# Zero products on TensorE ahead of the first weights, and the first loads of a decoder layer in halves

## The chip, the cores and the metric

The kernel runs on one core of one Trainium2 chip. The metric is the device time of one execution in microseconds (us). The core has five engines that run side by side, each with its own instruction queue: TensorE (PE in the profile, its weight loads as PEld), VectorE (DVE), ScalarE (ACT), GpSimd (POOL) and SyncE (SP). [...]DMA transfers between device memory and the on-chip buffers are issued from the queues of SP, ACT and POOL.

## What is computed

One post-norm decoder layer in float32 for 8 sequences of 112 tokens with 256 channels. The parts follow each other:

```
x = layernorm(x + self_attention(x))            # 16 heads of 64, w_qkv 256 x 3072, w_out 1024 x 256, bias
x = layernorm(x + cross_attention(x, context))  # 16 heads of 16, context of 375 rows, mask, biases
x = layernorm(x + moe(x))                       # 8 experts, hidden 512, each token to its best one,
                                                # and one shared expert for all tokens
```

The first thing that can be computed is the projection of x to queries and keys: `x @ w_qkv`, the columns 0 to 1023 for q and 1024 to 2047 for k. Only this beginning of the kernel is touched by the change.

## The kernel before, in words

The host lays x out transposed (`in_xT`, 256 x 896), so that the channel is the partition; 256 channels make two chunks of 128, called k (KD = 2). The three parts of `w_qkv` are three tiles `wq`, `wk`, `wv` of 128 partitions x 2 chunks x 1024 columns.

The order of the work is written out by hand. Inside `tc.manual_schedule()` each engine executes what the program issues, in program order; the tables FIRST, STEP, STEP6, STEP7 and LAST are lists of short words, and `step` runs them one after the other. A word such as `k6` or `u0-` is one piece: some matmuls into one PSUM tile and the copy out of it (`+` by DVE, `-` by ACT).

The beginning goes like this.

- Loads. `load` is SP's DMA start, `A.dma_start` is ACT's. L131 loads the columns of x of the first two sequences (both chunks in one transfer, 224 KB). `load_w(start, n, c, width)` (L128 and L129) loads `width` columns of q, k or v (n = 0, 1, 2) from column c, for both chunks. L132 to L138: q's columns 0 to 255 from ACT's queue, k's 0 to 255 from SP, q's 256 to 511 from ACT, k's 256 to 511 from SP, then from SP q's, k's and v's remaining halves of 512 columns each. After them SP issues the context of sequence 0, the cross-attention weights and biases, the rest of `xT` (L158), the residual x, the output weights and more (L153 to L167).
- Constants. POOL makes the identity for the transposes, a few small tiles and zeros in two wide tiles; DVE makes three tiny vectors (L177 to L180). TensorE has nothing to do before the first projection.
- First pieces. L559 and L560 run the four pieces k0 to k3 of `project(0, 0)`: k0 is q's columns 0 to 255, k1 is k's columns 0 to 255, k2 and k3 the same for columns 256 to 511. One piece is four calls of `nc.tensor.matmul` in `product` (L246 to L248): two column blocks of 128, called i here, each summed over the two chunks. Then ACT scales q into `qT` (L273), or DVE copies k into `kT` (L244). The trace shows two TensorE instructions for each such call in float32, so eight for a piece.
- Then the table FIRST: `k6 k4 u0- k5- k7+ s0 e0 s1 k3- ...`. Here k4 to k7 are the other halves of the projection of sequences 0 and 1, u0 is half of the values of sequence 0, s0 and s1 are the scores of the self attention. A later `k3` is already a piece of the next pair of sequences and reads the rest of `xT`.

All matmul pieces of this kind draw their PSUM tile from `m_tile` (L97), a pool with two buffers.

Eight sequences then go through the steps, with the self attention of one sequence laid between the cross attention of the one before. The loads of later contexts wait for a free buffer, so for TensorE's progress. The end (LAST) is the routing, the experts, the shared expert and the last norm.

Of the kernel before, what the change touches and what calls it, by code (L numbers as in the profile page):

```python
# [8 lines left out]
F32 = mybir.dt.float32  # L9
# [5 lines left out]
P = 128  # L15
# [38 lines left out]
def decoder_layer(  # L54
# [8 lines left out]
    nc = tc.nc  # L63
    B, S, D = x.shape
    NT = B * S
    S2 = ctxT.shape[1] // B
    KD = D // P
# [6 lines left out]
    E, _, H = upT.shape  # L74
# [14 lines left out]
    V, A, G = nc.vector, nc.scalar, nc.gpsimd  # L89
# [7 lines left out]
    def m_tile():  # L97
        return ps_m.tile([P, 512], F32, tag="mm", name="mm")
# [10 lines left out]
    ac = sa.enter_context(tc.tile_pool(name="ac", bufs=1))  # L109
# [3 lines left out]
    xT_sb = ac.tile([P, KD, NT], F32, name="xT_sb")  # L113
# [10 lines left out]
    load = nc.sync.dma_start  # L124
    xT_v = xT.rearrange("(k p) n -> p k n", p=P)
    w_v = w_qkv.rearrange("(k p) n -> p k n", p=P)

    def load_w(start, n, c, width):  # L128
        start(out=wqkv[n][:, :, bass.ds(c, width)], in_=w_v[:, :, bass.ds(n * INNER + c, width)])  # L129

    load(out=xT_sb[:, :, 0 : 2 * S], in_=xT_v[:, :, 0 : 2 * S])  # L131
    load_w(A.dma_start, 0, 0, 256)  # L132
    load_w(load, 1, 0, 256)
    load_w(A.dma_start, 0, 256, 256)
    load_w(load, 1, 256, 256)
# [426 lines left out]
    for s in range(B):  # L562
        if s + 1 < B:
            load_context(s + 1)
        if s in (1, 2):
            load(
                out=(xs_d if s == 1 else y_d)[:, :].rearrange("(t p) d -> p t d", p=P),
                in_=fill_sb.unsqueeze(1).to_broadcast([P, E * NT // P, D]),
# [409 lines left out]
```

## Time and profile before

| what | value |
|---|---|
| median of the 3 runs | 417.99 us (417.88 to 418.55) |
| the profiled execution's own time | 418.89 us |
| its span in the trace | 417.2 us |
| TensorE busy | 399.4 us, 96% of the span |
| VectorE, ScalarE, GpSimd busy | 58%, 45%, 18% |
| first TensorE instruction | 5.11 us after the span's start |

The span is what lies between the first and the last record of the trace; the profiled execution's own time is 1.7 us more. In the profile a line such as "5.11 3.36 PE L248 MATMUL ... x8" reads: from 5.11 us, for 3.36 us, eight matmuls issued by line 248; in brackets stands how long the engine had been idle and what released it. PEld is the loading of weights into the array, which runs beside matmuls. "128*128 128x224" means stationary 128 x 128, output 128 partitions x 224 columns. SPq and ACTq are the queues that issue DMAs.

### The profile page before, as it was taken

What the parts mean: (1) busy time and instruction counts of PE and PEld (TensorE: products, weight loads), DVE (VectorE), ACT (ScalarE), POOL (GpSimd) and SP (SyncE); (2) the same over time, 40 slices, a digit from 0 to 9 for tenths busy, and PEclk for the clock granted to TensorE, in tenths of its full rate; (3) what the DMA queues carried; (4) which work ended last, traced back from release to release, by engine and by line L of the source; (5) the groups of instructions that cost most, each with busy time, mean ns of one, the idle gap of its engine ahead of it and who ended that gap; (6) DMA issues with size and microseconds to landing.
All of it is one profiled execution on the core that took longest, in us unless ns stands there. A gap on an engine that the chain in (4) does not pass through costs nothing.

```text
span 417.2 us, 8496 instructions
## 1 busy us (share of the span) xinstructions
PE 399.4 (96%) x3347; PEld 311.2 (75%) x3347; DVE 239.9 (58%) x672; ACT 188.2 (45%) x476; POOL 75.3 (18%) x111
## 2 busy tenths in 40 slices
PE   5999999999999999999999999999999989999991
PEld 4877768967886887688678867867857559998670
DVE  0173585578458665865784587489487424223173
ACT  1232366455727554654567286577476221112000
POOL 3012112103012200221030112104100520000271
PEclk9999999999999999999999999999999999999998
DMA  8980298099010001000000100000694140995132
GB/s 273 309 224 0 78 376 293 4 362 353 26 37 2 2 1 38 2 2 8 31 2 2 38 0 2 2 2 2 218 373 167 46 142 4 304 358 174 45 107 60
DMA packets 38334, 46.61 MB, mean 112 GB/s; under 512 B 2181, under 2 KB 31378, under 8 KB 38290
## 3 DMA queue, kind: packets, MB, share of 16 engines
q1 hardware_dynamic: 36978, 43.66, 32.2%
q0 software_dynamic: 768, 1.84, 1.5%
q8 instruction: 28, 0.46, 0.5%
q10 hardware_dynamic: 544, 0.52, 0.4%
q14 instruction: 16, 0.13, 0.1%
HBM read 28.41 MB, written 17.60 MB: 110 GB/s over the span
## 4 chain that ended last, share of the span: by engine, by line
PE 86%; POOL 4%; issue 4%; DMA 3%; DVE 2%; ACT 0%; SPq 0%; POOLq 0%; DVEq 0%
PE mm L248 46%; PE pt L485 10%; PE sc L248 7%; PE sc L437 7%; PE mm L496 5%; PE sc L336 4%; PE mm L372 3%; PE pt L365 3%; POOL r L677 1%; POOL xs_d L664 1%; DMA wq<-in_w_qkv 1%; POOL rs L229 1%; PE pt L239 1%; DMA xs_d<-xres,place_i 1%; DMA xs<-xs_d 1%
## 5 line engine op out<-in xcount | busy, mean ns | idle before, releaser
L455 ACT ACTIVATE ex<-ex,nm 112x375 f32<-112x375 f32 x128 | 76.8, 601 | 47.3 <-DVE nm L451 46.5
L451 DVE CUSTOM_DVE_ANT_0 ex<-sc,cap 112x375 f32<-112x375 f32 x128 | 63.7, 545 | 10.0 <-PE sc L437 9.6
L485 PEld LDWEIGHTS pt<-ident,ex 112*125 112x125 f32 x384 | 50.9, 188 | 17.2 <-issue 10.0
L485 PE MATMUL pt<-ident,ex 112*125 112x112 f32 x384 | 55.1, 275 | 0.1
L244 ACT COPY exT<-pt 125x448 f32<-125x448 f32 x56 | 28.4, 528 | 29.1 <-PE pt L485 29.0
L358 POOL TENSOR_TENSOR pr<-pr,den 112x896 f32<-112x896 f32 x16 | 26.9, 1684 | 80.9 <-DVE den L357 44.2
L229 POOL TENSOR_TENSOR rs<-rs,mhalf 112x1 f32<-112x1 f32 x24 | 13.4, 560 | 144.6 <-DVE rs L228 144.5
L248 PE MATMUL mm<-xT_sb,wq 128*128 128x224 f32 x128 | 28.9, 373 | 5.1 <-DMA wq<-in_w_qkv 5.1
L248 PE MATMUL mm<-wv,xT_sb 128*112 128x512 f32 x64 | 31.1, 608 | 0.0
L248 PEld LDWEIGHTS mm<-xT_sb,wq 128*128 128x128 f32 x128 | 24.4, 199 | 8.5 <-DMA wq<-in_w_qkv 5.1
L437 PE MATMUL sc<-kc,qz 32*112 32x375 f32 x256 | 29.8, 519 | 0.1
L248 PE MATMUL mm<-wo,aoT 128*112 128x256 f32 x128 | 29.0, 380 | 0.0
L244 DVE COPY exT<-pt 125x448 f32<-125x448 f32 x40 | 24.8, 623 | 7.0 <-PE pt L485 6.5
L248 PE MATMUL mm<-xT_sb,wk 128*128 128x224 f32 x128 | 28.0, 364 | 0.0
L248 PEld LDWEIGHTS mm<-xT_sb,wk 128*128 128x128 f32 x128 | 24.8, 198 | 1.7 <-issue 0.5
L248 PE MATMUL mm<-wxv,cT 128*125 128x256 f32 x96 | 25.6, 389 | 0.0
L248 PEld LDWEIGHTS mm<-wo,aoT 128*112 128x112 f32 x128 | 22.0, 177 | 4.5 <-DVE aoT L244 0.2
L455 ACT ACTIVATION_READ_ACCUMULATOR ex<-ex,nm 112x1 f32 x128 | 24.1, 188 | 0.0
L248 PE MATMUL mm<-cT,wxk 128*128 128x375 f32 x64 | 23.2, 486 | 0.0
L244 DVE COPY prT<-pt 112x448 f32<-112x448 f32 x16 | 9.9, 621 | 20.7 <-PE pt L365 20.7
L496 PE MATMUL mm<-exT,vc 125*32 125x112 f32 x768 | 21.7, 261 | 0.0
L345 DVE TENSOR_REDUCE mx<-sc 112x8 f32<-112x896 f32 x16 | 17.4, 1088 | 5.8 <-PE sc L336 5.3
(156 smaller groups left out, 641.1 us busy)
## 6 DMA issues: line engine op xcount, KB each, us to landing
xs_d<-fill_sb SPq DMA_DIRECT2D x1, 7168.0 KB, 24.2
y_d<-fill_sb SPq DMA_DIRECT2D x1, 7168.0 KB, 24.9
wg<-in_gateT SPq DMA_DIRECT2D x9, 512.0 KB, 8.5
wu<-in_upT SPq DMA_DIRECT2D x9, 512.0 KB, 7.5
wd<-in_downT SPq DMA_DIRECT2D x9, 512.0 KB, 8.0
cT<-in_ctxT SPq DMA_DIRECT2D x8, 375.0 KB, 3.6
wv<-in_w_qkv SPq DMA_DIRECT2D x2, 512.0 KB, 7.8
wo<-in_w_out SPq DMA_DIRECT2D x1, 1024.0 KB
```

The lines of the kernel that those rows point to most:

```text
L229: G.tensor_tensor(rs[:n], rs[:n], mhalf[:n], ALU.pow)
L244: (V.tensor_copy if on == "+" else A.copy)(dst, src)
L248: nc.tensor.matmul(out_, lhsT, rhs, start=(i == 0), stop=(i == len(pairs) - 1))
L336: nc.tensor.matmul(sc[:S, j, bass.ts(c, S)], qT[rows, 4 * g + c, self.tok], kT[rows, 4 * g + c, self.tok], start=True, stop=True,)
L345: V.tensor_reduce(self.mx, scv, AX.X, ALU.max)
L358: G.tensor_tensor(pr, pr, den.unsqueeze(3).to_broadcast([S, 2, 4, S]), ALU.mult)
L365: nc.tensor.transpose(pt[:S, bass.ts(c, S)], self.pr[g][:, j, c, :], ident[:S, :S])
L437: nc.tensor.matmul(sc[i // 2][:S, i % 2, :S2], self.qz[rows, par, c, :], kc[rows, c, :], start=True, stop=True,)
L451: V.tensor_tensor_reduce(ex[:, i, :], self.sc[g][i // 2][:S, i % 2, :S2], cap, -1.0, BIG, ALU.add, ALU.min, nm[:, i : i + 1],)
L455: A.activation(ex[:, i, :], ex[:, i, :], AF.Exp, bias=nm[:, i : i + 1], scale=-1.0, accum_out=den[:, i, g % 2 : g % 2 + 1],)
L485: nc.tensor.transpose(pt[:JT, bass.ts(i, S)], self.ex[g][:, i, bass.ts(t, JT)], ident[:S, :S])
L496: nc.tensor.matmul(av[32 * i : 32 * i + 32, 0:S], vcs[self.b % 2][:, t, 4 * c + i, bass.ds(32 * par, 32)], self.exT[2 * c + par][:, t, bas ...
```

## The change

Ahead of all loads a tile of 128 x 128 zeros is allocated, VectorE fills it, and TensorE multiplies it with itself seven times into a PSUM tile of `m_tile` that nobody reads. Then the first loads are issued in smaller parts and in another order: q's first 256 columns become two transfers of 128 columns (both from ACT's queue), and the columns of x for the first two sequences become two transfers, one for each chunk (both from SP's queue). All other loads follow as they were. Nothing else in the kernel is changed.

```
-    load(out=xT_sb[:, :, 0 : 2 * S], in_=xT_v[:, :, 0 : 2 * S])
-    load_w(A.dma_start, 0, 0, 256)
+
+    zeros = ac.tile([P, P], F32, name="zeros")
+    V.memset(zeros, 0.0)
+    idle = m_tile()
+    for _ in range(7):
+        nc.tensor.matmul(idle[:, :P], zeros, zeros, start=True, stop=True)
+
+    load_w(A.dma_start, 0, 0, P)
+    for k in range(KD):
+        load(out=xT_sb[:, k, 0 : 2 * S], in_=xT_v[:, k, 0 : 2 * S])
+    load_w(A.dma_start, 0, P, P)
     load_w(load, 1, 0, 256)
     load_w(A.dma_start, 0, 256, 256)
     load_w(load, 1, 256, 256)
```

## The prediction

> **What bounds the kernel now.** I read the page first, then the chain of waits in order of time for the first 60 us, then the timeline of the first 20 us, then the tables by stretches of the start and of the end, and the waits of TensorE over the whole span. The page:
>
> ```profile
> PE 399.4 (96%) x3347; PEld 311.2 (75%) x3347; DVE 239.9 (58%) x672; ACT 188.2 (45%) x476; POOL 75.3 (18%) x111
> PE 86%; POOL 4%; issue 4%; DMA 3%; DVE 2%; ACT 0%; SPq 0%; POOLq 0%; DVEq 0%
> ```
>
> TensorE is busy 96% of the span and carries 86% of the chain that ends last: time taken off TensorE's own work or off its start comes off the end, unless something takes its place. Two pieces of the chain and two waits of TensorE tell where it starts:
>
> ```profile
> 0.81 4.25 DMA wq<-in_w_qkv
> 5.11 16.73 PE mm L248 x68
> ...
> PE mm L248 <- DMA wq<-in_w_qkv: 5.1, 1, 5.1
> PE pt L800 <- DMA xs<-xs_d: 1.1, 2, 0.9
> ```
>
> The first weights of q end the wait at 5.11; after that TensorE waits for a DMA only near the end, 1.1 us. What it does from 5.11 on is the key to this change:
>
> ```profile
> 5.11 3.36 PE L248 MATMUL mm<-xT_sb,wq 128*128 128x224 f32 x8 [5.11 <-DMA wq<-in_w_qkv]
> 8.26 2.79 PE L248 MATMUL mm<-xT_sb,wk 128*128 128x224 f32 x8
> 10.89 1.68 PE L248 MATMUL mm<-xT_sb,wq 128*128 128x224 f32 x8
> 12.40 1.68 PE L248 MATMUL mm<-xT_sb,wk 128*128 128x224 f32 x8
> ```
>
> Four pieces of eight equal matmuls start at 5.11, 8.26, 10.89, 12.40, and the fifth at 13.91. The distances are 3.15, 2.63, 1.51, 1.51. No wait is shown inside, and yet the first two take 1.64 and 1.12 us more: 2.76 us. In the first, an instruction takes about 0.37 us, from 10.70 on 0.19: TensorE runs at half rate for 5.6 us. The clock column doesn't say so:
>
> ```profile
> 5.00:8.00 3.00, 2.89 (x8) 2.63 (x9) 0.00 (x0) 0.00 (x0) 0.00 (x0) 1.00 1.08 368
> ...
> 412.00:414.00 2.00, 0.00 (x0) 0.00 (x0) 0.00 (x0) 0.00 (x0) 0.00 (x0) 0.82 0.26 71
> 414.00:417.20 3.20, 0.00 (x0) 0.00 (x0) 0.00 (x0) 0.00 (x0) 0.00 (x0) 0.50 0.02 4
> ```
>
> (columns: length, PE, PEld, DVE, ACT, POOL, granted clock, DMA share, GB/s.) It shows 1.00 at 5 to 8, where the intervals are doubled, but at the end, with TensorE idle from 408.2, it falls to 0.50 (at 413.3 in finer stretches). So 0.5 is this engine's clock when it has been idle, and 1.00 at the start I read as "no record yet".
>
> [...]
>
> **The change part by part.**
>
> *Zeros.* VectorE's fill of 128x128: POOL's of the same shape took 0.205 us, DVE has nothing before its first instruction at 1.55. From 0.8, so ready at about 1.0. Seven calls are 14 instructions (a piece of four calls shows eight). The nearest row is wxq's projection, 128*128 with 112 columns, eight in 0.88 us (46.19 to 47.07): 0.11 us each at full clock, 0.13 scaled to 128 columns, doubled while cold: 0.22 to 0.25, so 3.1 to 3.5 us, from about 1.1 to 4.2 or 4.6. This lies in the 5.1 us in which TensorE waits, so it costs nothing if the first operands arrive at 4.5; without that cover it would be 3.3 us. DVE's three tiny vectors move by 0.2 us; they are read by the queries at about 46. The unread PSUM tile shifts the turn of the two buffers; the piece that gets it back is on TensorE too, in order behind it, so nothing.
>
> [...]
>
> *The halves.* The first matmul now needs 128 KB of q and 112 KB of x, instead of 256 and 224. In fine stretches DMA moves 292 GB/s at 3.0 to 3.4 and some 375 after it; summed to 5.07 that is about 830 KB, of which 490 are the two tiles and the rest other loads. Half of it is reached at 4.0. The bounds are 4.0 and 5.07; I take 4.5. But this serves only the first of four calls: the second needs the other chunk of x, the third the other half of q, and these come when the undivided ones came, about 5.0 to 5.1; later, up to 5.8, if transfers with half as long rows (512 bytes, which no row of this trace has) get a smaller share beside SP's. So the halves themselves move one or two instructions, 0.2 to 0.4 us, and nothing if the clock is up, since the next tile then decides.
>
> *What is late next.* k1 needs wk's first part. It was issued at 1.33 and landed at 6.1 (4.8 us later); SP now issues one transfer more ahead of it (0.46 us), so 6.1 to 6.6. Before, it was wanted at 8.26, so it was hidden; now it decides. After it the weights come faster than they are used: 256 KB each 0.7 us against 1.51 us of work. q's second half landed near 8.6 and is wanted about 11; v's first landed near 11.4, wanted about 14; the rest of xT landed at 10.04 + 8.6 = 18.6, wanted at 23.53, now 20.7. Slack of about 2 us each. The SP queue's own waits (SPq L157, L158, ... one landing each) are those of eight transfers in flight; the two added ones are early in that row, so from bk on each issue waits for the same landing as before. ACT issues one DMA more (0.5 us), so its table load ends at 3.7, not 3.2; its first use was at 8.50, now about 6.5.
>
> [...] I charge the issue of 0.46 us only.
>
> *Sum.* Clock up by about 5: k0 from 4.5, ends with q's second half near 6.2; k1 from 6.4, then 1.51 each: k6 at 10.95 against 13.91, gain 2.95. Clock up at 7.2: k0 from 4.5 cold, 8 x 0.37, to 7.5; k6 at about 11.95, gain 2.0. The middle is 2.5 us of span. Against the profiled execution's 418.89 that is 416.4; the median of the runs is 0.9 lower. If that difference is profiling, 415.5; if it is a shorter cold stretch in those runs, the gain against them shrinks to about 2 and the time is 416. I take 415.6. Nothing after 21 us takes it back: loads there wait for buffers that TensorE frees, so they move along.
>
> **The rivals.**
>
> 1. *The clock rises before real work, all of it kept*: 3.0 to 3.3 us less, 414.7 to 415.0. For it: the row of 2.76 us. Against it: wk becomes the wait.
> 2. *Zeros don't lift the clock, or too late*: products of zeros might not count as activity, or count only until the gap before the first weights. Then only the halves remain: 0 to 0.4 us of gain, 417.6 to 418.0. For it: 2 us of work, up to 7.2, weren't enough in the row. Against: a gap of under 1 us.
> 3. *Slower: the zeros outlast the loads.* If weight loads don't run beside products of so few columns while cold (a cold weight load shows 337 ns), 14 x 0.337 = 4.7 us from 1.2 ends at 5.9, 0.8 behind the 5.11 of before. It decides if the clock rises no sooner after that: +0.8, 418.8. A pair must cost over 0.28 us for it; wxq's row at 0.11 speaks against it, doubled it is 0.22.
> 4. *The transfers take it back*: 512-byte rows at half the rate delay all that is behind them by some 0.7 us and wk's first part to 7.3: gain 1 to 1.7, 416.3 to 417.
>
> **How the numbers follow.** A measurement of this kernel tells about 0.2%, 0.84 us, from no change. The clock up in time or partly (forecast and rival 1): 0.68, of which 0.25 for rival 1. Rival 4: 0.12, nearly all faster than 417.15. Rival 2: 0.11, mostly within 0.2%. Rival 3 and other losses: 0.09. Faster 0.81, same 0.10, slower 0.09. The range of 414.5 to 417.3 takes in the forecast, rival 1 and rival 4 and leaves rivals 2 and 3 out.
>
> **What would show it.** Right: 14 instructions on zeros from about 1.1, ended by 4.6; the first real matmul at 4.0 to 5.0; the fifth piece (k6) at 11 to 12 instead of 13.91; a new wait of TensorE for wk of under 1 us; pieces of 1.51 us from the second on. Wrong: k0 and k1 still 3.1 and 2.6 us apart (rival 2), zeros ending after 5.1 (rival 3), waits for wq or xT over 1 us behind k1 (rival 4), or k6 earlier by 2 us and the last pieces of the trace not.

## The result, and the profile after

The changed kernel takes 417.1 us (median of 22 runs) against 418.35 us of the kernel before (22 runs, the three shown among them): ratio 0.9969, interval 0.9962 to 0.9977, so about 1.3 us faster. One execution of each kernel was slow (2,282 and 2,288 us), and the ratio leaves both out. 415.6 was predicted, 2.4 us less than the three runs' 417.99. The sign was right and the size was half of what was forecast.

The profiled execution took 417.91 us, its span is 416.1. The page's first row, and the timeline of TensorE:

```profile
PE 401.2 (96%) x3361; PEld 312.9 (75%) x3361; DVE 240.0 (58%) x673; ACT 187.5 (45%) x476; POOL 75.3 (18%) x111
```

```profile
1.13 3.35 PE L136 MATMUL mm<-zeros 128*128 128x128 f32 x14 [1.13 <-DVE zeros L133]
...
4.27 2.73 PE L257 MATMUL mm<-xT_sb,wq 128*128 128x224 f32 x8
...
7.90 1.75 PE L257 MATMUL mm<-xT_sb,wk 128*128 128x224 f32 x8 [0.90 <-DMA wk<-in_w_qkv]
...
9.49 1.68 PE L257 MATMUL mm<-xT_sb,wq 128*128 128x224 f32 x8
...
11.01 1.68 PE L257 MATMUL mm<-xT_sb,wk 128*128 128x224 f32 x8
...
12.52 1.68 PE L257 MATMUL mm<-xT_sb,wq 128*128 128x224 f32 x8
```

The 14 zero products run from 1.13 to 4.48, the first piece begins at 4.27 (ends are modelled, so the two groups overlap by 0.21 us), ends at 7.0, and then TensorE waits 0.90 us for k's first weights. The fifth piece, k6, starts at 12.52; before it was 13.91. So 1.39 us are gained at the start, in this pair of executions. The new wait stands in the chain of the changed kernel too:

```profile
1.75 6.02 DMA wk<-in_w_qkv
7.77 0.14 issue
7.90 12.55 PE mm L257 x60
```

These weights were issued at 1.75 and landed at 7.77; before, issued at 1.33, they landed at 6.1. The tables by stretches show what DMA did meanwhile, here before and after:

```profile
3.80:4.20 0.40, 0.00 (x0) 0.00 (x0) 0.00 (x0) 0.00 (x0) 0.15 (x1) 1.00 1.07 369
4.20:4.60 0.40, 0.00 (x0) 0.00 (x0) 0.00 (x0) 0.00 (x0) 0.00 (x0) 1.00 1.09 384
```

```profile
3.80:4.20 0.40, 0.40 (x4) 0.40 (x3) 0.00 (x0) 0.00 (x0) 0.15 (x1) 1.00 0.42 91
4.20:4.60 0.40, 0.40 (x3) 0.40 (x2) 0.00 (x0) 0.00 (x0) 0.00 (x0) 1.00 0.66 207
```

In the same 0.4 us from 3.8, 369 GB/s before and 91 after. This fall in what DMA moves is called the dip below.

**The clock, read exactly.** The column of the granted clock doesn't show the start (it has no record before the first change). But the trace's clock records give the moment at which the full rate begins, and the time from there to the fall at the end: 10.50 us and 402.773 us in the kernel before, 6.39 and 402.773 in the changed one. 402.773 is 118 times 3.4133. All 16 profiles of this study have 118 or 119 such steps between the first rise and the last fall; one of them (both_x1_act) also falls and rises in between, at 9.69 and 13.10 after a rise at 6.28, one step each. Where these steps lie against the span's start differs from execution to execution: the first rise, less whole steps, was at 0.26 in the kernel before and at 2.98 in the changed one. A stretch of 3.413 us between two such places is called a window below.

### The profile page after: what moved, and what is told of

The parts are those of the page before. It is cut to its first block, busy times and chain, and to the rows that moved or that the text cites. A ratio compares the mean times of both kernels' runs of the same rounds, so it can differ in the third digit from the quotient of the medians.

```text
span 416.1 us, 8528 instructions
## 1 busy us (share of the span) xinstructions
PE 401.2 (96%) x3361; PEld 312.9 (75%) x3361; DVE 240.0 (58%) x673; ACT 187.5 (45%) x476; POOL 75.3 (18%) x111
## 4 chain that ended last, share of the span: by engine, by line
PE 86%; POOL 4%; issue 4%; DMA 3%; DVE 2%; ACT 0%; SPq 0%; POOLq 0%; DVEq 0%
PE mm L257 45%; PE pt L494 10%; PE sc L257 7%; PE sc L446 7%; PE mm L505 5%; PE sc L345 4%; PE mm L381 3%; PE pt L374 3%; POOL r L686 1%; DMA wk<-in_w_qkv 1%; POOL xs_d L673 1%; POOL rs L238 1%; PE pt L248 1%; DMA xs_d<-xres,place_i 1%; PE pt L809 1%
## 5 line engine op out<-in xcount | busy, mean ns | idle before, releaser
L257 PE MATMUL mm<-xT_sb,wk 128*128 128x224 f32 x128 | 26.9, 354 | 0.9 <-DMA wk<-in_w_qkv 0.9
L257 PEld LDWEIGHTS mm<-xT_sb,wk 128*128 128x128 f32 x128 | 23.7, 190 | 2.6 <-PE mm L257 1.2
```

The costliest lines, as they stand in the source:

```text
L257: nc.tensor.matmul(out_, lhsT, rhs, start=(i == 0), stop=(i == len(pairs) - 1))
```

## Experiments

All times are ratios to the kernel before on the same chip, with 95% intervals. The table puts the profiled executions together: when the full rate begins, when k's first piece (k1) and k6 start, and the profiled execution's own time.

| kernel | full rate | k1 | k6 | us |
|---|---|---|---|---|
| before | 10.50 | 8.26 | 13.91 | 418.89 |
| changed | 6.39 | 7.90 | 12.52 | 417.91 |
| changed_again | 5.74 | 6.56 | 11.18 | 416.77 |
| zeros_only | 4.19 | 6.73 | 11.27 | 416.33 |
| halves_only | 9.24 | 7.53 | 13.00 | 418.06 |
| zeros_x_halves | 6.59 | 7.07 | 11.61 | 416.59 |
| zeros_w_halves | 4.85 | 6.56 | 11.10 | 416.48 |
| zeros9_only | 6.35 | 7.31 | 11.85 | 416.47 |
| zeros12_w_halves | 6.47 | 7.96 | 12.50 | 417.09 |
| both_merged | 4.04 | 6.88 | 11.50 | 416.43 |
| merged_again | 6.58 | 7.10 | 11.64 | 416.67 |
| both_q2_sp | 4.29 | 6.50 | 11.12 | 416.00 |
| w_merged | 6.80 | 7.33 | 11.87 | 416.91 |
| both_wide_mid | 5.15 | 6.70 | 11.31 | 416.73 |
| merged_k2_act | 4.66 | 8.19 | 12.81 | 417.70 |
| both_x1_act | 6.28, 13.10 | 9.73 | 15.94 | 420.94 |

In every row the time less the start of k6 is 404.6 to 405.6, over a range of 4.8 us in k6. Matmul by matmul from k6 on, 13 of the 16 traces run in step to within 0.02 us up to 320 us (behind that, near the routing, they part by some 0.2). So what is won or lost before k6 is nearly all still there at the end. But three traces lose something near 21 us: changed_again 0.47, both_wide_mid 0.14, both_q2_sp 0.07. What they wait for is shown at changed_again.

### The two parts alone, and each split alone

zeros_only leaves the loads undivided:

```
     for _ in range(7):
         nc.tensor.matmul(idle[:, :P], zeros, zeros, start=True, stop=True)
+    load(out=xT_sb[:, :, 0 : 2 * S], in_=xT_v[:, :, 0 : 2 * S])
+    load_w(A.dma_start, 0, 0, 256)
-    load_w(A.dma_start, 0, 0, P)
-    for k in range(KD):
-        load(out=xT_sb[:, k, 0 : 2 * S], in_=xT_v[:, k, 0 : 2 * S])
-    load_w(A.dma_start, 0, P, P)
```

> The zero products alone; the first loads as before, undivided. Theory (the halves make k's first weights late: they landed at 7.77 in the changed kernel, at 6.1 before, and so eat the gain of the clock): k's weights land near 6.1 again, the first real matmul is back near 5.1, k6 starts near 11.5 to 12.0 instead of 12.52, and the gain against before is 1.7 to 2.4 us (ratio 0.994 to 0.996), more than the changed kernel's 1.3. Rival A (the zeros bring little, the halves bring what gain there is): k6 at 13 to 14, ratio 0.998 to 1.001. Rival B (a gap in TensorE's activity between zeros and weights keeps the clock down for one more window): lift at 8 to 10, ratio 0.997 to 0.999.

Measured: 0.9987 (0.9969 to 1.0006), and its 14 runs lie in two groups, five at 416.0 to 416.5 and nine at 418.2 to 419.2. The profile is one of the first group:

```profile
1.13 3.28 PE L136 MATMUL mm<-zeros 128*128 128x128 f32 x14 [1.13 <-DVE zeros L133]
5.11 1.78 PE L255 MATMUL mm<-xT_sb,wq 128*128 128x224 f32 x8 [0.71 <-DMA wq<-in_w_qkv]
6.73 1.68 PE L255 MATMUL mm<-xT_sb,wk 128*128 128x224 f32 x8
```

Here full rate began at 4.19, before any real work: nothing but zero products had run on TensorE until then. The first piece then takes 1.62 us to the next, nearly the 1.51 of full rate. Between 4.41 and 5.11 TensorE is idle, which proves to matter below. The theory's 0.994 to 0.996 fits the group of five alone. Rival A's range holds the ratio, but not two groups, nor a k6 at 11.27. The group of nine has the ratio of rival B; its own clock is in no trace.

halves_only removes the zero products:

```
-    zeros = ac.tile([P, P], F32, name="zeros")
-    V.memset(zeros, 0.0)
-    idle = m_tile()
-    for _ in range(7):
-        nc.tensor.matmul(idle[:, :P], zeros, zeros, start=True, stop=True)
```

> The halves alone, no zero products. Theory: first real matmul near 4.3, then at half rate; k's weights land near 7.8, which is after the first piece has ended at 7.3, so k1 starts at 7.8 with the clock still low, and loses another 1.3 us there: k6 within 0.5 us of the 13.91 of before, ratio 0.998 to 1.001. Rival A (the halves carry the gain): k6 near 12.5, ratio about 0.997.

Measured: 0.9986 (0.9974 to 0.9997), the ratio that the theory had. Its k6 was to be within 0.5 us of 13.91; it is at 13.00, halfway to rival A's 12.5. Rival A's 0.997 lies just outside the interval.

```profile
3.77 3.35 PE L251 MATMUL mm<-xT_sb,wq 128*128 128x224 f32 x8 [3.77 <-DMA wq<-in_w_qkv]
7.53 2.61 PE L251 MATMUL mm<-xT_sb,wk 128*128 128x224 f32 x8 [0.41 <-DMA wk<-in_w_qkv]
9.98 1.68 PE L251 MATMUL mm<-xT_sb,wq 128*128 128x224 f32 x8
```

The first operands are there at 3.77 instead of 5.11, but at half rate (3.35 us for the first eight matmuls, 1.68 for eight from 9.98 on), and k's weights are late here too (7.5). The halves alone are worth at most 1.1 us, and more likely 0.6.

zeros_x_halves keeps q's first weights whole, zeros_w_halves keeps x whole:

```
# zeros_x_halves
+    load_w(A.dma_start, 0, 0, 256)
-    load_w(A.dma_start, 0, 0, P)
     for k in range(KD):
         load(out=xT_sb[:, k, 0 : 2 * S], in_=xT_v[:, k, 0 : 2 * S])
-    load_w(A.dma_start, 0, P, P)
# zeros_w_halves
     load_w(A.dma_start, 0, 0, P)
-    for k in range(KD):
-        load(out=xT_sb[:, k, 0 : 2 * S], in_=xT_v[:, k, 0 : 2 * S])
+    load(out=xT_sb[:, :, 0 : 2 * S], in_=xT_v[:, :, 0 : 2 * S])
     load_w(A.dma_start, 0, P, P)
```

> Zero products, and only x in two transfers; q's first weights undivided. Tells which of the two splits makes k's weights late. If it is SP's extra issue (k's first weights issued at 1.75 and not 1.33): they land at 7 to 7.8 here too, ratio about 0.997. If it is the 512-byte rows of q on the other queue: they land at 6.1 to 6.6, ratio 0.994 to 0.996.

> Zero products, and only q's first weights in two transfers; x undivided. If SP's extra issue makes k's weights late: they land at 6.1 to 6.6 here, ratio 0.994 to 0.996. If it is the 512-byte rows or the third transfer of ACT's queue: 7 to 7.8, ratio about 0.997.

Measured: 0.9952 (0.9933 to 0.9971) and 0.9950 (0.9932 to 0.9969). In neither does TensorE wait for k's weights. So neither SP's later issue (1.75 in zeros_x_halves) nor q's 512-byte rows make them late by themselves. In the packet records of the changed kernel a 512-byte packet took 27 ns, a 1024-byte one 46 (medians): 17% more for each byte.

```profile
4.49 2.23 PE L256 MATMUL mm<-xT_sb,wq 128*128 128x224 f32 x8
6.56 1.68 PE L256 MATMUL mm<-xT_sb,wk 128*128 128x224 f32 x8
8.07 1.68 PE L256 MATMUL mm<-xT_sb,wq 128*128 128x224 f32 x8
```

This row of zeros_w_halves is what had been predicted for the change: first piece at 4.49, k1 at 6.56, k6 at 11.10.

### How many zeros

zeros9_only is zeros_only with nine; zeros12_w_halves is zeros_w_halves with twelve:

```
-    for _ in range(7):
+    for _ in range(9):      # zeros9_only; range(12) in zeros12_w_halves
```

> Nine zero products, loads undivided: TensorE then stays active until the weights land near 5.1, where seven left it idle from 4.41 to 5.11. Theory (the clock is released at the end of a window of 3.41 us in which TensorE was active for more than some share between 60 and 88%, and the idle 0.7 us spoils those windows that hold it whole): the runs are no longer in two groups (416.0 to 416.5 and 418.2 to 419.2 with seven); all lie between 415.8 and 417.2, ratio 0.994 to 0.996. Rival (the undivided loads themselves cost the slow group its 2.5 us): still two groups, ratio 0.998 to 1.000.

Measured: 0.9949 (0.9932 to 0.9966), six runs from 415.7 to 417.2: the second group is gone. The loads are undivided here too, so they are not its cause; what went with the group is the idle 0.7 us.

```profile
1.13 4.21 PE L136 MATMUL mm<-zeros 128*128 128x128 f32 x18 [1.13 <-DVE zeros L133]
5.13 2.34 PE L255 MATMUL mm<-xT_sb,wq 128*128 128x224 f32 x8
```

> Only q's first weights in halves, and twelve zero products instead of seven: 24 instructions, which at half rate last until 6.4 (1.13 + 24 x 0.22), about 1.9 us behind the first weights at 4.5. Tells what zeros that outlast the loads cost. If TensorE's time is what counts: with the clock up at 4.5 to 7.9 the zeros end at 5.5 to 6.4 and k0 at 7.0 to 7.9, so 0.5 to 1 us worse than seven: ratio 0.996 to 0.9985. If k's weights at 6.1 to 6.6 are the bound: within 0.3 us of seven, ratio 0.995.

Measured: 0.9959 (0.9944 to 0.9975). The zeros occupy TensorE until 6.41, when the first piece starts; k6 is at 12.50 against 11.10 with seven. In the trace the surplus costs 1.4 us, by the ratios 0.4, which the intervals don't separate. Part of the 1.4 is the clock: full rate began at 6.47 here and at 4.85 there. Had it begun at 4.85, the last seven of the 24 would have taken some 0.8 us less (an estimate, from the 0.22 us that a zero product took at half rate, and the 0.11 of wxq's matmuls at full rate in the kernel before).

The profiles show how busy TensorE was ahead of each rise. In the window that ended with the first rise it was active for 85% of the time in both_merged (1.13 to 4.04), 88% in halves_only, 90% in zeros_only, more elsewhere. Windows with no rise at their end had up to 66%: w_merged from 1.13 to 3.39, 60% in halves_only, merged_again and zeros_x_halves, 58% in the kernel before, 54% in the changed one. Ahead of a first rise no profile has a window between 66 and 85%. One of zeros_only that held the whole idle stretch would have 79%; that this was too little in the group of nine is my reading, which no trace shows.

The 14 runs of zeros_only agree with it. Each run's record has its span and its mean granted clock. In the traces the clock is recorded below 1 only behind its last fall (0.50 from 413.27 on in the kernel before), so the two give the moment of that fall, and with it the place of the windows, to about 0.4 us (an estimate, from three digits of the mean clock). The five fast runs had their windows begin at 0.6 to 1.9 us (counted from the span's start, less whole steps of 3.413), the nine slow ones at 1.8, at 3.1 to 3.3 and at 0.1 to 0.65. If 79% was too little and 85% enough, the zeros and the real work of this profile lifted the clock in time only if a window began between about 0.5 and 1.6 us (an estimate from its 1.13, 4.41 and 5.11).

### Why k's first weights are late with both splits

both_merged joins ACT's second and third transfer, both_q2_sp moves the third to SP:

```
# both_merged
-    load_w(A.dma_start, 0, P, P)
+    load_w(A.dma_start, 0, P, 3 * P)
     load_w(load, 1, 0, 256)
-    load_w(A.dma_start, 0, 256, 256)
# both_q2_sp
     load_w(load, 1, 0, 256)
-    load_w(A.dma_start, 0, 256, 256)
+    load_w(load, 0, 256, 256)
```

> The changed kernel, but q's columns 128 to 511 come in one transfer of ACT's queue (384 columns) instead of two; so more bytes are issued by 1.3 us. Theory (with both splits the first four small transfers are through by 3.8, and what was issued behind them starts slowly, so DMA runs at 91 to 264 GB/s from 3.8 to 5.0 and k's first weights land at 7.8): no such dip here, k's first weights at 6.1 to 6.8, ratio 0.994 to 0.996. Rival (512-byte rows or SP's later issue by themselves): the dip and 7.5 to 7.8 stay, ratio 0.997.

Measured: 0.9943 (0.9928 to 0.9958), k's weights at 6.8, no dip (380 GB/s from 3.8 to 4.2).

```profile
4.17 2.04 PE L256 MATMUL mm<-xT_sb,wq 128*128 128x224 f32 x8
6.88 1.75 PE L256 MATMUL mm<-xT_sb,wk 128*128 128x224 f32 x8 [0.67 <-DMA wk<-in_w_qkv]
...
3.80:4.20 0.40, 0.40 (x5) 0.40 (x4) 0.00 (x0) 0.00 (x0) 0.15 (x1) 1.00 1.00 380
```

> The changed kernel with q's third transfer (columns 256 to 511) issued from SP, behind k's first weights: ACT then has two transfers, as in both_merged, but only 480 KB are issued by 1.3 us. If the bytes in flight decide: the dip stays, k's first weights land at 7 or later or only a little sooner since nothing shares the engines with them, ratio 0.996 to 0.998. If ACT's third transfer decides: no dip, k's first weights at 6.1 to 6.8, ratio 0.994 to 0.996.

Measured: 0.9953 (0.9939 to 0.9966). The dip is there (179 GB/s from 3.8, 159 from 4.2), as it was to be if the bytes in flight decide, and yet k's weights land by 6.4 (k1 at 6.50 after a wait of 0.53). ACT's queue moved its last packet at 3.94, so it shared the engines with nothing of SP's behind that. So the dip alone isn't what makes them late.

both_x1_act moves x's second chunk to ACT's queue, both_wide_mid cuts ACT's three transfers 128, 256, 128:

```
# both_x1_act
-    for k in range(KD):
-        load(out=xT_sb[:, k, 0 : 2 * S], in_=xT_v[:, k, 0 : 2 * S])
+    for k, start in ((0, load), (1, A.dma_start)):
+        start(out=xT_sb[:, k, 0 : 2 * S], in_=xT_v[:, k, 0 : 2 * S])
# both_wide_mid
-    load_w(A.dma_start, 0, P, P)
+    load_w(A.dma_start, 0, P, 2 * P)
     load_w(load, 1, 0, 256)
-    load_w(A.dma_start, 0, 256, 256)
+    load_w(A.dma_start, 0, 3 * P, P)
```

> The changed kernel, but the second chunk of x is issued from ACT's queue, between the two halves of q's first weights; SP then issues k's first weights at 1.28 instead of 1.75. Theory (too little in flight at 3.8): 608 KB instead of 480 are issued by 1.8 us, the dip is smaller, k's first weights land at 6.1 to 6.8, ratio 0.994 to 0.996. Rival (the splits as such): k's first weights at 7.3 or later, ratio 0.997.

Measured: 1.0050 (1.0035 to 1.0065), 2 us slower than the kernel before. q's second half, now ACT's third transfer, was issued at 1.8 and landed at 8.8:

```profile
4.28 1.81 PE L257 MATMUL mm<-xT_sb,wq 128*128 128x224 f32 x4
8.85 1.08 PE L257 MATMUL mm<-xT_sb,wq 128*128 128x224 f32 x4 [2.76 <-DMA wq<-in_w_qkv]
9.73 3.19 PE L257 MATMUL mm<-xT_sb,wk 128*128 128x224 f32 x8
```

The idle 2.76 us also cost the clock: it rose at 6.28, fell at 9.69 after a window with 25% of activity, and rose again at 13.10. So k1 and the first instructions of k2 ran at half rate once more (0.58 us in k1 for a matmul that took 0.35 at full rate). My expectation (0.994 to 0.996, some 2 us faster) was off by 4 us, and the rival's 0.997 by more than 3.

> The changed kernel with ACT's three transfers cut 128, 256 and 128 columns instead of 128, 128 and 256: as many transfers, in the same order, but 608 KB issued by 1.3 us instead of 480. If the bytes in flight when the first transfers are through decide: the dip of DMA between 3.8 and 5.0 is gone or smaller, k's first weights land at 6.1 to 7.0, ratio 0.994 to 0.996. If the number of transfers on the queues decides: dip and 7.5 to 7.8 stay, ratio 0.997 or worse.

Measured: 0.9967 (0.9955 to 0.9979). DMA dips later, 188 and 180 GB/s from 5.0 to 6.0, after the 608 KB are through. k's weights land at 6.6 in the profile, after a wait of 0.3 us, and ACT's third transfer needs 5.9 us for 128 KB. So each side has one half: the landing is the first's, the ratio the second's.

w_merged is both_merged with x undivided:

```
-    for k in range(KD):
-        load(out=xT_sb[:, k, 0 : 2 * S], in_=xT_v[:, k, 0 : 2 * S])
+    load(out=xT_sb[:, :, 0 : 2 * S], in_=xT_v[:, :, 0 : 2 * S])
```

> A candidate: seven zero products, x undivided, q's first 512 columns as 128 and 384. SP then issues k's first weights at 1.33, ACT 512 KB by 1.3. Theory: no dip, first real matmul near 4.5, k's first weights at 5.5 to 6.2, never waited for; q's second part near 5.8 is; k6 at 11.0 to 11.6, ratio 0.993 to 0.996, like both_merged. Rival (the bigger second part of q comes too late for the first piece): a wait over 1 us for wq, ratio 0.996 to 0.998.

Measured: 0.9960 (0.9947 to 0.9974); no dip, no wait for k's weights, k6 at 11.87, with the clock up only at 6.80.

Last, the changed kernel and both_merged once more on one chip, and both_merged with a third transfer put on ACT's queue:

```
# merged_k2_act, against both_merged
-    load_w(load, 1, 256, 256)
+    load_w(A.dma_start, 1, 256, 256)
```

> The changed kernel once more, unaltered, beside both_merged on the same chip. Theory (k's first weights are late in it as a rule): they land at 7.3 to 8.2 again, the dip of DMA lies between 3.8 and 5.0 again, ratio 0.996 to 0.998. Rival (the late landing was one execution's): 6.1 to 6.8, ratio as both_merged.

Measured: 0.9966 (0.9953 to 0.9979), as the first time. But in this profile k's weights are there when TensorE asks for them at 6.56, while DMA dips as before (220 GB/s from 3.8 to 4.6):

```profile
4.28 2.40 PE L257 MATMUL mm<-xT_sb,wq 128*128 128x224 f32 x8
6.56 1.75 PE L257 MATMUL mm<-xT_sb,wk 128*128 128x224 f32 x8
```

So the dip was there in two of two profiles of this kernel, and in halves_only, and the late landing was not: 7.8 once, at most 6.6 once.

Yet with k6 at 11.18 this execution took 416.77 us, about the median of its five runs (416.87). Something is lost later. The chain of waits shows it:

```profile
3.72 6.79 DMA wk<-in_w_qkv
10.51 0.02 issue
10.52 10.64 DMA xT_sb<-in_xT
21.16 0.14 issue
21.30 9.72 PE mm L257 x40
```

Here SP's issue of the rest of x waits for the landing of k's columns 512 to 1023, at 10.51. The rest of x then needs 10.64 us and lands at 21.16, while TensorE is done with the work in front of it by 20.87 (an idle 0.43 us, and k3's matmuls 0.5 us late). In the kernel before, it was issued at 10.04, landed at 18.6 and was wanted at 23.53. In both_wide_mid and both_q2_sp it lands at 20.96 and 20.66, also just behind its need. So a kernel that gets through its start sooner meets this load next, and k's first weights are not the only ones that can take the gain back.

> both_merged once more, beside the changed kernel on the same chip: theory 0.7 to 1.3 us faster than the changed kernel (ratio 0.993 to 0.9955), k's first weights at 6.4 to 6.9. Rival: no difference between the two.

Measured: 0.9958 (0.9946 to 0.9970) on the chip on which the changed kernel had 0.9966. The 0.7 us expected between them are not seen; 0.3 is, inside both intervals.

> both_merged, with k's columns 256 to 511 issued as a third transfer of ACT's queue instead of SP's. If what is issued in the first two turns (736 KB here) decides: no dip before 5, k's first weights at 6.1 to 6.9, ratio 0.993 to 0.9955. If three transfers on ACT's queue behind two short ones on SP's make the dip: it returns, k's first weights at 7.3 or later, ratio 0.997.

Measured: 0.9964 (0.9951 to 0.9978), and in the profile k's weights at about 8.0:

```profile
4.28 2.11 PE L256 MATMUL mm<-xT_sb,wq 128*128 128x224 f32 x8
8.19 1.75 PE L256 MATMUL mm<-xT_sb,wk 128*128 128x224 f32 x8 [1.81 <-DMA wk<-in_w_qkv]
...
3.80:4.20 0.40, 0.40 (x4) 0.40 (x3) 0.00 (x0) 0.00 (x0) 0.15 (x1) 1.00 0.99 312
```

DMA had no dip before 5, with 736 KB issued in two turns, and the weights were late all the same. So too few bytes in flight is not what makes them late here. In the packet records a few of k's 1024-byte packets still come from SP's queue between 5.5 and 7.5 while the transfer behind them already moves. Which DMA engines moved those packets the records don't name.

What the runs show together: with both x and q's first weights split and three or more transfers on ACT's queue, one that is issued third on its queue, near 1.8 us, can land late. In four profiles the one that is waited for did, at 7.8, 7.5, 8.0 and 8.8 (k's, and q's second half in both_x1_act); in both_wide_mid ACT's third did, at 7.7, and k's was in time; in changed_again k's was in time. With x or q's first weights whole, or only two transfers on ACT's queue, k's first weights landed by 6.8 in seven profiles. The kernels with zeros sort by it (zeros_only, with its idle stretch, aside): 0.9943 to 0.9960 without, 0.9964 to 0.9969 with, and 1.0050. Most of the intervals overlap across the two sets. In the first set SP issues the rest of x at 9.6 to 10.1 (10.76 in both_q2_sp), in the second at 10.5 to 11.9, so part of the sorting can be that load's. Why the last packets are late is open.

## Why the prediction was half right

**Right.** The bound and the way through: TensorE's chain, nearly all of a gain at k6 comes out at the end (404.6 to 405.6 us behind it in 16 profiles). The half rate behind the first two pieces (0.37 us from one matmul to the next instead of 0.19, until full rate at 10.50). The zeros: 14 instructions from 1.13 to 4.48, where 1.1 to 4.2 or 4.6 were said, free of cost. With nothing but zeros before it, full rate began at 4.19 in zeros_only, so rival 2 falls. The first real matmul at 4.27 (4.0 to 5.0). Rival 3 falls: a zero product took 0.22 us, not 0.34, and even twelve calls weren't slower than before.

**Wrong, in two terms of the sum.** The sum's two times for the rise of the clock, about 5 and 7.2, are shown by no run of the changed kernel: full rate began at 6.39 and at 5.74 in its two profiles, and between 4.04 and 6.80 in the other kernels with zeros. Take 405.05 us from k6 to the end, the mean of the table. The forecast's middle, k6 at 11.45, is then 416.5. The forecast was 415.6 and the median is 417.1: 0.9 us were lost on the way from the middle to the forecast, and 0.6 us on the way from the middle to the measurement.

First, the 0.9: the step "the median of the runs is 0.9 lower. If that difference is profiling, 415.5", with 415.6 taken. It is not profiling, it is the place of the clock's windows. The profiled executions lie among the others (416.77 with a median of 416.87 in changed_again, 416.59 with 416.57 in zeros_x_halves, 416.43 with 416.16 in both_merged). And the 84 runs of the kernel before that were made beside the experiments, sorted by the place of their windows (read from span and clock as for zeros_only) into quarters of 3.413 us, have medians of 418.94, 417.92, 418.05 and 418.47 us. The profiled execution of before, with full rate from 10.50 (0.26 behind whole steps), belongs to the first quarter, and took 418.89. It was one with a long cold stretch, k6 at 13.91; the median of 22 runs, 418.35, stands for 13.3. The prediction wrote this down as the other possibility, gave it too little weight, and summed it wrong: how fast the kernel before ran doesn't change what the changed one takes, so that branch stays at 416.4, a gain of 1.6 against 417.99, and not "about 2 and the time is 416".

Second, the 0.6: the loads behind the first ones were given too much slack. "It was issued at 1.33 and landed at 6.1 (4.8 us later); SP now issues one transfer more ahead of it (0.46 us), so 6.1 to 6.6": the issue was later by 0.42 us, as charged, but the landing was 7.77 in the first profile, 6.0 us after the issue. The clock was up at 6.39, in time for nearly all; yet k1 started at 7.90, not at 6.4 to 7.5. "Slack of about 2 us each": in the second profile k's first weights were in time, and the rest of x, carried over as landing at 18.6, landed at 21.16 and cost 0.5 us. "Nothing after 21 us takes it back" is wrong for that execution. How the 0.6 us of the typical run divides between the two, and whether the place of the windows has a part in it, stays open, and so does why the landings spread. The kernels with seven zeros that remove one split or ACT's third transfer reach k6 at 11.1 to 11.9, and 0.9943 to 0.9960: 1.7 to 2.4 us of gain, close to the forecast.

Rival 4 had the right place and size (gain of 1 to 1.7), but by the wrong mechanism: not the short rows, which zeros_w_halves has too. That one transfer more costs its issue of 0.46 us alone fitted the kernel before, with x and q whole: there the 256 KB parts of wq and wk landed at 5.1, 6.1, 6.5 and 7.3, 0.4 to 1.0 us apart. It didn't hold for four short transfers with two more on their heels (7.77 for k's first weights).

The halves were worth more than "one or two instructions", in a way that was not foreseen: they bring the first work to the end of the seven zero products and so close the idle 0.7 us. Without them seven zeros failed in nine runs of 14 (read from the times and the place of the windows). Nine zeros do the same without splitting anything, 0.9949 against the change's 0.9969 and 0.9966, with intervals that overlap.

## What to carry to other kernels

Full rate began anywhere from 4.04 to 10.50 us in these 16 profiles, and at another place in two profiles of one kernel (6.39 and 5.74), so one profile is one draw: compare medians of many runs, and compare the profile's early stretch with the chain behind it before an offset is called profiling. Warm TensorE up without a pause until the real operands are there; a pause of 0.7 us in front of them spoiled nine runs of 14 here, while a surplus of five products cost 0.4 us by the ratios (0.9959 against 0.9950). And splitting first loads moves the ones behind them (k's first weights from 6.1 to 7.77 in the first profile): look where the third transfer of each queue lands, not only the first, and take a slack measured in one execution as one draw too.

## What the runs showed of the hardware

- From the first rise of TensorE's clock to its last fall there were 118 or 119 times 3.413 us in each of 16 profiles, and the first rise was at 4.04 to 10.50 us. The windows that ended with a first rise had 85% of activity or more, those before it without a rise up to 66%, and one of 25% ended with a fall (both_x1_act, at 9.69). In zeros_only full rate began at 4.19, behind nothing but products of zeros.
- The profile's clock column reads 1.00 until the first record, also where matmuls take double (0.37 us instead of 0.19).
- In both_x1_act the third transfer on ACT's queue, 128 KB, took 7.0 us from issue to landing, while the first, 128 KB, took 2.8 and the second, 112 KB, 3.6. In the five other profiles with both splits and three on ACT's queue, SP's third took 4.7 to 6.3.
